# PixArt-style two-layer block on one core: first loads on two queues, and the second FFN's third and fourth elements prepared inside the last attention step

## The chip, the cores and the metric

The kernel runs on one core of one Trainium2 chip. The metric is the device time of one execution in microseconds (us). All data are float32; the matmuls run in float32 too.

## The reference

Sixteen batch elements of 256 tokens by 256 channels go through two layers. Each layer has self-attention, cross-attention and an FFN, each with a modulated layer norm ahead of it and a residual behind it. Cut to what matters:

```python
# layer 0 (16 heads of 64, rotary embedding on q and k; inner width 1024)
attn_in = adaln(x, cond, ...g1, b1)
x = attn(attn_in, attn_in, sa_wq, sa_wkv, sa_wo, sa_bo) + x
cross_in = adaln(x, cond, ...g1, b1)
x = attn(cross_in, ln(context), ca_wq, ca_wkv, ca_wo, ca_bo) + x
ffn_in = adaln(x, cond, ...g2, b2)
x = gelu(ffn_in @ ff_w1 + ff_b1) @ ff_w2 + ff_b2 + x
# layer 1 (16 heads of 16; six modulation vectors from silu(cond) @ Wmod + bmod)
x = x + attn_self(ln(x) * (1 + sc1) + sh1) @ Wos + bos
x = x + attn_cross(ln(x) * (1 + sc2) + sh2, context) @ Woc + boc
x = x + gelu((ln(x) * (1 + sc3) + sh3) @ W1 + b1) @ W2 + b2
```

Here `ln` is the layer norm over the last axis, `adaln(x, c) = ln(x) * (1 + c @ gw + gb) + (c @ bw + bb)`, and `attn` ends with the output product.

## The kernel before

Six phases run one after the other: layer 0's self-attention, cross-attention and FFN, then layer 1's. In each phase a loop runs over the 16 elements (`b`, a "job" each, whose key is phase_element); an attention job has two steps (`s` = 0, 1), an FFN job four. All of x stays in SBUF, one tile per element (`x0` to `x15`), and so do the weights of the running phase.

The order of work on every engine is the order in which the program issues it (`manual_schedule` for TensorE, VectorE, ScalarE, GpSimd and SyncE): each engine executes its own list in order, and waits in it for semaphores of the others. The short names of the profile are PE (TensorE's matmuls), PEld (its weight loads), DVE (VectorE), ACT (ScalarE), POOL (GpSimd), SP (SyncE, which issues the DMAs; ScalarE issues some too). DMAs share eight semaphores in turn, so that a DMA also waits for the landing of the one issued eight before it.

PSUM is one tile of eight banks, addressed by number. Attention steps of layer 1 use four banks from `at = 4 * s`: the next element's or the FFN's first products at `at`, the output product of the element before at `at + 1`, the two attention products (`layer1_sums`, e = 0, 1) at `at + 2` and `at + 3`. The FFN takes banks in turn by `next_bank()`; the first FFN product of phase 5 is put at bank 4 within the last attention step (`ffn_products`), and the ones after it take bank 7, 0, 1, 2 and so on.

How an element enters a phase, in four moves, each some steps ahead of its use:

- `prepare_moments`: mean and variance (VectorE: two L350, two L352, L354), and rstd by a power on GpSimd (L356).
- `prepare_norm`: `normalized` (VectorE, two L364 into the one buffer `xh`), then `turn` (two 32x32 stream transposes, L374, into `blocks`, and four DMAs, L379, that write `turned` to DRAM), then `add_bias` (GpSimd, two L452: the output bias is added to x).
- `prepare_fetch`: four DMAs (L389) that read `turned` back as `fetched`, transposed.
- `prepare_input`: `affine`, which applies the modulation to `fetched` and makes `hT` (chunk 0 on ScalarE, L422; chunk 1 on GpSimd, L426, or ScalarE, L424).

The layer-1 attention's softmax sums are inverted by `invert` (a VectorE reciprocal, L773), spread and multiplied in by `normalize` (VectorE L781, GpSimd L782); `finish` is the output product (TensorE, 16 products of four matmuls of 32 columns) and its addition to x (VectorE, L1044).

The FFN's elements 0 and 1 are computed plainly (`ffn_hidden`: 4 quarters of 16 products each). From element 2 on, pairs of elements (2 and 3, 4 and 5, ...) share a Strassen-like scheme of seven products: `fold_input` makes the four sums `inner` from both elements' hT (L839 to L842, for the first pair on VectorE), `block_products` uses them, and the output side uses sums of the weights, `output_w` (`fold_output_weights`, VectorE, L913 to L916, at element 1, step 2). All four sums need the hT of both elements.

The start: x0, the packed vectors `rows`, weights and tables are loaded by SP in one sequence; ScalarE's queue loads only the first modulation's weights. `condition` computes the sigmoid, transposes cond and `rows` on TensorE, with `idle_products` (matmuls of the identity that are not used) between them; then come the first modulation (L186 to L194), the first element's norm (`xh_first`), its four transposes, hT, and the first products of phase 0 (L82). Each of the two wk and wq loads of the `"first"` and `"last"` part covers half the heads; `load_first` is called between them and puts rope, the value weights, x1, x2, fold and mask after the first half.

## Time and profile before

| what | value |
|---|---|
| time, median of 3 runs | 2160.07 us (2159.74 to 2161.54) |
| profiled execution, its own time | 2160.07 us |
| its span, first to last instruction | 2158.3 us |
| PE busy | 2143.1 us (99%) |
| DVE, POOL, ACT busy | 1645.4, 1319.5, 877.6 us |
| mean granted TensorE clock | 0.999 |

The span is the stretch from the first to the last instruction; the time of an execution has 1.8 us more around it. A row of the order of time gives the start in us from the span's begin, the duration, engine, line, operation, out<-in tiles, shapes and count; neighbours of one kind are merged. In brackets stands how long the engine was idle before it and what ended that. Matmuls are pipelined, so that the next group can start before the last one's end. A product of the kernel appears as two matmuls per 32-column strip.

### The profile page before, as it was taken

To read this page: it belongs to the slowest core of one execution; us is meant where nothing else is said; L and a number is where in the kernel's file an instruction comes from. 1 tells how busy PE (TensorE), PEld (TensorE's weight loads), DVE (VectorE), ACT (ScalarE), POOL (GpSimd) and SP (SyncE) were. 2 spreads that over 40 slices of the span, in tenths; PEclk is the share of its full clock that TensorE was granted. 3 is DMA by queue.
4 is the path that set the end of the run, shared out by engine and by line. 5 is a ranking of instruction groups with operands and counts; after the bars stand their busy time and mean duration, and the time that the engine had idled before them with its cause. 6 is when DMAs were issued, how large, how long until landed. Compare 5 with 4: busy or idle time off the path is not lost.

```text
span 2158.3 us, 109746 instructions
## 1 busy us (share of the span) xinstructions
PE 2143.1 (99%) x50000; PEld 1423.2 (66%) x50000; DVE 1645.4 (76%) x3008; ACT 877.6 (41%) x1377; POOL 1319.5 (61%) x1234
## 2 busy tenths in 40 slices
PE   9999999999999999999999999999999999999998
PEld 5666666666666666666666678886566655656787
DVE  5877777777787889888888777865777777777865
ACT  3333333333323332333323333433666666664342
POOL 5867767767768777686776766662322233235773
PEclk9999999999999999999999999999999999999999
DMA  6110110110133221212212033221212232223221
GB/s 195 30 38 23 27 39 22 27 39 23 30 93 84 75 60 35 59 43 45 58 35 62 24 77 91 54 51 22 64 39 43 55 93 62 62 48 76 73 66 39
DMA packets 307027, 117.65 MB, mean 55 GB/s; under 512 B 243364, under 2 KB 289784, under 8 KB 306424
## 3 DMA queue, kind: packets, MB, share of 16 engines
q1 hardware_dynamic: 306008, 110.02, 20.5%
q8 instruction: 393, 6.44, 1.3%
q14 instruction: 82, 0.67, 0.1%
q10 hardware_dynamic: 544, 0.52, 0.1%
HBM read 77.14 MB, written 33.29 MB: 51 GB/s over the span
## 4 chain that ended last, share of the span: by engine, by line
PE 94%; DVE 2%; POOL 2%; DMA 1%; issue 1%; SPq 0%; ACT 0%; DVEq 0%; POOLq 0%; ACTq 0%
PE banks L82 60%; PE banks L657 16%; PE banks L724 10%; PE banks L740 5%; PE banks L593 2%; PE banks L502 1%; POOL qk L622 1%; POOL raw L713 1%; POOL folded L1003 0%; DVE x L957 0%; DMA spread<-sums_seen 0%; DVE m L614 0%; DMA rows<-in_rows 0%; POOL folded L926 0%; DMA turned<-blocks 0%
## 5 line engine op out<-in xcount | busy, mean ns | idle before, releaser
L670 ACT ACTIVATE pr<-banks 128x1024 f32<-128x1024 f32 x576 | 487.4, 938 | 423.4 <-PE banks L657 219.4
L622 POOL TENSOR_TENSOR qk<-m,m 128x512 f32<-128x512 f32 x256 | 378.4, 1498 | 214.6 <-DVE m L614 203.9
L614 DVE TENSOR_TENSOR m<-banks,rope 128x512 f32<-128x512 f32 x512 | 319.7, 678 | 33.9 <-PE banks L82 22.4
L676 DVE TENSOR_TENSOR both<-pr 128x1024 f32<-128x1024 f32 x128 | 169.4, 1323 | 101.8 <-ACT pr L670 100.1
L657 PE MATMUL banks<-qk 32*64 32x256 f32 x8192 | 239.5, 378 | 0.8 <-POOL qk L622 0.5
L724 PE MATMUL banks<-pr,v 128*32 128x256 f32 x4096 | 236.2, 379 | 0.0
L731 ACT COPY raw<-banks 128x512 f32<-128x512 f32 x128 | 75.1, 587 | 391.6 <-PE banks L724 379.4
L657 PEld LDWEIGHTS banks<-qk 32*64 32x64 f32 x8192 | 184.6, 131 | 59.8 <-issue 29.1
L724 PEld LDWEIGHTS banks<-pr,v 128*32 128x32 f32 x4096 | 133.4, 110 | 100.3 <-issue 16.8
L452 POOL TENSOR_TENSOR x<-x,bo_b 128x256 f32<-128x256 f32 x96 | 73.0, 779 | 164.8 <-DVE xh L364 164.8
L782 POOL TENSOR_TENSOR oT<-oT,spread 128x256 f32<-128x256 f32 x64 | 45.7, 735 | 206.5 <-DVE spread L781 206.5
L713 POOL TENSOR_TENSOR raw<-raw,spread 128x512 f32<-128x512 f32 x128 | 162.4, 1302 | 13.1 <-DMA spread<-sums_seen 13.1
L682 DVE STREAM_TRANSPOSE squares<-both 128x1024 f32<-128x1024 f32 x128 | 158.7, 1240 | 2.2
L689 DVE TENSOR_REDUCE rows<-squares 128x32 f32<-128x1024 f32 x128 | 155.1, 1212 | 1.7
L1003 POOL TENSOR_TENSOR folded<-raw,raw 128x512 f32<-128x512 f32 x90 | 141.8, 1604 | 2.4
L82 PE MATMUL banks<-hT,wk_sa 128*32 128x256 f32 x2048 | 134.7, 381 | 0.2 <-ACT hT L422 0.2
L82 PE MATMUL banks<-hT,wq_ca 128*32 128x256 f32 x2048 | 134.4, 379 | 0.0
L740 PE MATMUL banks<-pr,wide_v 128*32 128x256 f32 x2048 | 134.4, 379 | 0.0
L82 PE MATMUL banks<-hT,wq_sa 128*32 128x256 f32 x2048 | 133.9, 379 | 0.0
L657 PE MATMUL banks<-q,k 32*64 32x256 f32 x4096 | 128.3, 382 | 0.2 <-issue 0.2
L957 DVE TENSOR_TENSOR x<-banks,x 128x256 f32<-128x256 f32 (+2 forms) x150 | 79.6, 531 | 56.2 <-PE banks L82 49.8
L657 PEld LDWEIGHTS banks<-q,k 32*64 32x64 f32 x4096 | 87.5, 131 | 38.2 <-issue 14.3
(248 smaller groups left out, 4033.0 us busy)
## 6 DMA issues: line engine op xcount, KB each, us to landing
turned<-blocks SPq DMA_DIRECT2D x380, 64.0 KB
fetched<-turned SPq DMA_DIRECT2D x380, 64.0 KB
spread<-sums_seen SPq DMA_DIRECT2D x128, 128.0 KB
x<-in_x SPq DMA_DIRECT2D x16, 256.0 KB
fetched_c<-turned_c SPq DMA_DIRECT2D x64, 64.0 KB
cT<-in_ctx_turned SPq DMA_DIRECT2D x16, 256.0 KB
out<-x SPq DMA_DIRECT2D x15, 256.0 KB
ctx<-in_ctx SPq DMA_DIRECT2D x16, 192.0 KB
```

The source lines that it names most:

```text
L82: nc.tensor.matmul(out[cut], lhsT[:, cut], rhs, start=start, stop=stop, **more)
L614: nc.vector.tensor_tensor(m, pq, rope[:, s : s + 1, :].to_broadcast([P, 2, N]), ALU.mult)
L622: nc.gpsimd.tensor_tensor(r, x, y, (ALU.subtract, ALU.add)[out])
L657: nc.tensor.matmul(banks[64 * g : 64 * g + 64, at + h, t * N : (t + 1) * N], lhs, rhs, start=(half == 0 and (t == 0 or job["layer"] == 1)) ...
L670: nc.scalar.activation(pr[:, one], sc[:, one], AF.Exp, scale=0.125 if job["layer"] == 0 else 0.25)
L676: nc.vector.tensor_tensor(both, pr[:, :, 0, :], pr[:, :, 1, :], ALU.add)
L682: nc.vector.transpose(job["squares"].rearrange("p b k -> p (b k)"), job.pop("both").rearrange("p h n -> p (h n)"))
L689: nc.vector.tensor_reduce(job["rows"][:, u, :], job.pop("squares"), AX.X, ALU.add)
L713: nc.gpsimd.tensor_tensor(part, part, spread[:, u : u + 1, :].to_broadcast([P, 2, N]), ALU.mult)
L724: nc.tensor.matmul(o[32 * h : 32 * h + 32, half, :], v[:, t, col : col + 32], pr[:, h, t, :], start=(t == 0), stop=(t == NT - 1),)
L740: nc.tensor.matmul(o[32 * h : 32 * h + 32], v[:, t, 4 * c + h, 32 * e : 32 * e + 32], pr[:, h, t, :], start=(t == 0), stop=(t == NT - 1),)
L1003: eng.tensor_tensor(folded[m], *sums[m])
```

## The change

It has two parts.

The first loads. SP now issues cond, rows, x0, fold and mask. wk and wq of the first half and rope go to ScalarE's queue, issued by a call inside `condition`, behind the sigmoid and ahead of the exponential. The value weights, x1, x2, the second half of wk and wq, the output bias and weights and the other x tiles come on SP in this order, issued in the program after the first element's transposes. `xh_first` lies in the buffer of the value weights (`wpool`, tag `wv`) and not in `xh`; so the load of the value weights waits for the transposes that read it.

The border to the second FFN. In the last step of the last attention element (layer 1, s = 1, next is the FFN; `border`), `prepare_norm` of the FFN's element 2 and `prepare_moments` of its element 3 are issued after the first of the two attention products (e = 0) and not after both, or in the FFN's first step. In the FFN's element 0, step 0, element 3's norm, transposes and bias come first, and `invert` and `normalize` of the last attention element move to the end of step 1. The output product of that element (`finish(jobs[j - 2])`) moves from element 1's step 0 to its step 2, after that step's products.

On the engines' lists this means: PE has element 1's first 48 products in a row, then the 16 of the output product, then the last 16 of element 1. VectorE has element 2's norm and transposes and element 3's moments ahead of the last two reads of the second attention product (L754, L759, e = 1) and of the addition of element 14's output (L1044); the reciprocal comes after element 3's transposes, and the addition of element 15's output after element 4's norm and transposes. GpSimd has element 3's rstd ahead of element 1's hT, and element 3's bias ahead of `normalize`. SP writes element 3's `turned` before it fetches element 2's. The numbers of instructions on the engines stay the same, but for the three loads that move from SP to ScalarE.

```diff
-    def condition():
+    def condition(load):
         sig = work.tile([NB, D], F32, tag="inv", name="sig")
         nc.scalar.activation(sig, cond, AF.Sigmoid)
+        load()
...
-    def load_layer0_attention(kind, part, between=None):
+    def load_layer0_attention(kind, part, eng=nc.sync):
...
-            nc.sync.dma_start(out=wk, in_=wkv_src[:, :, halves[i]])
-            nc.sync.dma_start(out=wq, in_=chunked(a[f"{kind}_wq"])[:, :, halves[i]])
+            eng.dma_start(out=wk, in_=wkv_src[:, :, halves[i]])
+            eng.dma_start(out=wq, in_=chunked(a[f"{kind}_wq"])[:, :, halves[i]])
             w[f"wk{i}"], w[f"wq{i}"] = wk, wq
-            if between is not None and i == 0:
-                between()
...
-    def load_first():
-
-        nc.sync.dma_start(out=rope, in_=a["rope"])
-        load_phase(0, "values")
-        for b in range(1, 3):
-            load_x(b)
-        for dst, name in ((fold, "fold"), (mask, "mask")):
-            nc.sync.dma_start(out=dst, in_=a[name])
...
+    nc.sync.dma_start(out=rows, in_=a["rows"])
     load_x(0)
-    nc.sync.dma_start(out=rows, in_=a["rows"])
-    for part in ("first", "last", "early", "output"):
-        load_phase(0, part)
-    for b in range(3, NB):
-        load_x(b)
-    silu = condition()
+    for dst, name in ((fold, "fold"), (mask, "mask")):
+        nc.sync.dma_start(out=dst, in_=a[name])
+
+    def load_first():
+
+        load_phase(0, "first")
+        nc.scalar.dma_start(out=rope, in_=a["rope"])
+
+    silu = condition(load_first)
     jobs[0]["hraw"] = banks[:, 6:8, 0:N]
     found = moments(xs[0], "first")
-    xh = normalized(xs[0], found, D, "first")
+    xh = normalized(xs[0], found, D, "first", wpool, "wv")
...
+    load_phase(0, "values")
+    for b in range(1, 3):
+        load_x(b)
+    for part in ("last", "early", "output"):
+        load_phase(0, part)
+    for b in range(3, NB):
+        load_x(b)
     idle_products(2)
...
-            if b == 0 and s == (1 if layer0 else 0):
+            if b == 0 and s == 1 and layer0:
                 prepare_moments(third)
...
                 elif b == 0:
+                    prepare_norm(third)
                     prepare_fetch(after)
-                    invert(prev)
-                    third["turned"] = turn(
-                        normalized(xs[third["b"]], third.pop("moments"), D, third["key"]), 4, third["key"]
-                    )
-                    normalize(prev)
-                    add_bias(third)
-                if b == 1 and not layer0:
-                    finish(jobs[j - 2], next_bank())
...
+            if s == 1 and b == 0 and not layer0:
+                invert(prev)
+                normalize(prev)
             if s == 2:
+                if b == 1 and not layer0:
+                    finish(jobs[j - 2], next_bank())
...
+            border = nxt["kind"] == "ffn" and s == 1
             for e in range(2):
                 layer1_sums(job, s, e, at + 2 + e)
+                if border and e == 0:
+                    prepare_norm(third)
+                    prepare_moments(jobs[j + 4])
                 if s == 1:
                     finish(prev, at + 1, (e,))
...
             else:
-                prepare_norm(third)
+                if not border:
+                    prepare_norm(third)
                 prepare_input(after)
```

More of the change, by code (lines that the diff above doesn't have):

```diff
@@ L357, in moments, with normalized @@
         return mv, rstd
-    def normalized(src, found, width, name):
+    def normalized(src, found, width, name, pool=work, tag="xh"):
         mv, rstd = found
-        xh = work.tile([P, NT, width], F32, tag="xh", name=f"xh_{name}", bufs=1)
+        xh = pool.tile([P, NT, width], F32, tag=tag, name=f"xh_{name}", bufs=1)
         for t in range(NT):
@@ L1073, in fast @@
     phases = [
-        {"layer": 0, "kind": "attn", "cross": False, "load": lambda part: load_layer0_attention("sa", part, load_first),
+        {"layer": 0, "kind": "attn", "cross": False, "load": lambda part: load_layer0_attention("sa", part, nc.scalar if part == "first" else nc.sync),
          "mod_load": lambda: layer0_modulation(1)},
```

## The prediction

> **What bounds the kernel now.** I read the page first, then TensorE's waits, then the order of time on TensorE and VectorE around the two longest waits.

> ```profile
> PE 2143.1 (99%) x50000; PEld 1423.2 (66%) x50000; DVE 1645.4 (76%) x3008; ACT 877.6 (41%) x1377; POOL 1319.5 (61%) x1234
> ```

> TensorE (PE) is busy for 2143.1 of 2158.3 us. Both parts of the change add and remove no matmul, so they can give back only idle time, 15.2 us in all. Where it lies, the waits of PE tell (microseconds in total, times, longest):

> ```profile
> PE banks L82 <- DVE inner L840: 4.2, 1, 4.2
> PE banks L154 <- DMA rows<-in_rows: 1.3, 1, 1.3
> PE banks L138 <- POOL neg_half L93: 1.3, 1, 1.3
> ```

> The first lies at the start of the second FFN, the second and third in the first 6 us. The change touches the first and the second. PE's order of time at the start (start, duration, line, form, count, idle before):

> ```profile
> 3.02 1.22 PE L138 MATMUL banks<-ident 128*128 128x256 f32 x2
> 5.58 0.37 PE L154 MATMUL banks<-ident,rows 68*128 68x68 f32 x1 [1.34 <-DMA rows<-in_rows]
> 7.69 1.08 PE L186 MATMUL banks<-mod_a,condT 128*32 128x128 f32 x16
> 10.29 1.04 PE L138 MATMUL banks<-ident 128*128 128x256 f32 x4
> 11.48 0.85 PE L82 MATMUL banks<-hT,wk_sa 128*32 128x256 f32 x12 [0.15 <-ACT hT L422]
> ```

> PE is free at 4.24 and waits for rows until 5.58. All up to the first real product at 11.48 follows from there: modulation, its copy and transpose, five small VectorE steps, the affine hT.

> PE and its weight loads at the second FFN's start:

> ```profile
> 1948.44 1.05 PE L82 MATMUL banks<-wo_b,oT 128*32 128x256 f32 x16
> 1949.63 7.12 PE L82 MATMUL banks<-hT,w_b 128*32 128x256 f32 x128
> 1956.86 2.19 PE L82 MATMUL banks<-wo_b,oT 128*32 128x256 f32 x32
> 1958.87 6.23 PE L82 MATMUL banks<-hT,w_b 128*32 128x256 f32 x112
> ```
> ```profile
> 1949.63 3.40 PEld L82 LDWEIGHTS banks<-hT,w_b 128*32 128x32 f32 x68 [0.62 <-DVE sums L759]
> ```

> The reader is to see two things. PE stops when the line at 1958.87 ends, 1965.09, until the folded inputs are there at 1969.28. And at 1949.63 it already waits for VectorE's L759: the FFN's second quarter for element 0 is written to bank 7, where the last attention product (layer1_sums, e=1, bank at+3 with at=4) lies until L759 has read it. VectorE (DVE) at that place:

> ```profile
> 1949.10 0.47 DVE L759 SCALAR_TENSOR_TENSOR sums<-banks,mask,sums 128x256 f32<-128x256 f32 x1
> ...
> 1950.17 0.72 DVE L364 TENSOR_SCALAR xh<-x,mv,rstd 128x256 f32<-128x256 f32 x2
> ...
> 1952.46 0.28 DVE L354 TENSOR_SCALAR ve<-mv 128x2 f32<-128x2 f32 x1
> 1952.65 1.74 DVE L773 RECIPROCAL sums<-sums 128x256 f32<-128x256 f32 x1
> ...
> 1959.12 0.69 DVE L1044 TENSOR_TENSOR x<-banks,x 128x512 f32<-128x512 f32 x1 [1.60 <-PE banks L82]
> ...
> 1961.06 1.23 DVE L913 TENSOR_TENSOR output_w_L_xcond_b<-w_b 128x512 f32<-128x512 f32 x1
> ...
> 1968.80 0.43 DVE L840 TENSOR_TENSOR inner<-hT,inner 128x256 f32<-128x256 f32 x1
> ```

> **Part 1, the first loads.** rows goes ahead of x0 on SP's queue, issued at 1.18 instead of 1.64. By the landings in the trace cond (issued 0.72, same queue) took 1.9 us, x0 3.4 us (to 4.63), rows 3.9 us (to 5.54, behind x0's 256 KB). With 34 KB and only cond ahead, rows needs between 1.9 and 3.0 us and is there by 3.1 to 4.2. PE reaches L154 at 4.24, so the whole 1.34 us goes. The value is 1.34; bounds 0.9 (rows still dragged) and 1.34 for this step.

> What is late next: x0, now issued at 1.64. If it keeps its 3.45 us it lands at 5.1. The moments and the norm take from 6.14 to 8.94 today, 2.80 us, so xh would be complete at 7.9. PE's transposes of it begin at 9.43 today, 8.09 after the change: covered by 0.2 us, and 0.3 us more lie between the transposes' end (10.47) and the last addend (10.77).

> The three loads put on ScalarE's queue (wk, wq, rope) are issued behind the sigmoid, from about 3.1 us, at 0.45 to 0.49 us each as its two loads today: done at 4.6, then the table load (1.28) and the exponential (0.20), 6.1; the modulation's copy needs ScalarE at 7.5 (8.84 less 1.34). No cost. wk and wq landed at 8.36 and 10.07; they are needed at 10.1 and 11.0. They start a microsecond later but have the same bytes ahead and no longer the values, rope and x1 interleaved. No cost, 0.5 us if wq slips to 11.5. SP's next load, the values, waits for the last transpose (xh lies in their buffer), about 9.1, and with it wait x1, x2 and all later loads. Values took 1.28 us per 512 KB (12.01 to 13.29); 2 us of latency and two such transfers give 13.7, x1 14.3. PE wants the values at 17.0 (18.42 today), VectorE wants x1 at 15.0 (16.42). Covered. SP's first turned block stands behind thirteen x loads that end at 23.9 to 24.5; element 1's hT came at 35.86 and PE wants it at 39.42, a cover of 3.6 us against at most 2.

> The clock: the same idle product took 0.5 us a piece from 5.75 and 0.26 from 10.29 (4 in 1.04), and the change falls near 10.07. With the gap gone PE is dense from 3.02 on, not 5.58. I add 0.1 us (0, if the fast clock comes when it did, to 0.4, if it comes before the modulation; then x0 ends the stage). [...]

> Part 1: 1.34 + 0.1, **1.4 us gained** (0.9 to 1.7).

> **Part 2, elements 2 and 3.** Element 2's norm and element 3's moments move ahead of the last half step's two reads of bank 7 (L754, L759). On VectorE that is 9 instructions: two L364, two L374, two L350, two L352, one L354. Today they run from 1950.17 to the reciprocal's start at 1952.65, 2.48 us. Their inputs are there after L759 of e=0, which ends at 1947.96: rstd of element 2 is ready at 1947.48. So they run 1947.88 to 1950.36, L754 and L759 follow (0.40 start to start, then 0.47) to 1951.23, and PE begins at 1951.29 instead of 1949.63. **The moved work sits in front of what frees bank 7: 1.66 us lost** (the 0.73 us that VectorE idles ahead of L754 today, for PE's e=1 product, is filled by it and taken off already).

> Then PE runs without a stop: element 0's 48 products, 48 of element 1, at 0.108 us (7.12 less 0.19 for the last one's tail, over 64) to 1961.66. The output product of the last attention element (16 products, 1.73) ends at 1963.39; with the tail 1963.58. Its operand, normalized by POOL behind the reciprocal, is ready near 1956.7: cover 5 us. Today that product waits for POOL; 0.3 us ahead of it and 0.28 inside vanish, which this count holds already. 24 products more, and PE stands at the folded inputs at 1965.98.

> What is late next is VectorE. It adds that output (L1044, 0.07 us after PE's tail: 1963.65), 0.60 to the next, then L913 to L916. L913 took 1.23 us beside POOL's adds of L452 and the like ones behind it 0.69; POOL has nothing left to do then, so I take 0.69: L913 1964.25 to 1964.94, L914 from 1964.97, L915 1965.58, L916 1966.18, the first inner sum 1966.79 to 1967.21, the second 1967.24 to 1967.66; PE at 1967.72. [...]

> The DMAs: SP issues element 2's four blocks at 1949.3 (2.63), element 3's at 1953.2 (2.6), element 2's fetch at 1955.9 (1.70), element 3's when its last block has landed. A block took 2.1 to 3.7 us: 1957.7 to 1959.0. Fetched (1.7, and 1.9 for the last): 1961 to 1962.2. ScalarE makes element 3's hT behind its GELUs and element 2's hT, by 1964.8; VectorE wants it at 1966.79. Two us of cover, so L379's earlier place gives nothing beyond this.

> Part 2: 1969.28 less 1967.72, **1.56 us gained** (0.9 to 2.0); without the wait on bank 7 it would be 3.2.

> **Sum.** Nothing behind either place has a fixed date: the rest of the chain is PE itself. The profiled execution took 2160.07 us (span 2158.3 and 1.8 around it) and is also the median of the three (2159.74 to 2161.54). 2160.07 - 1.4 - 1.56 = **2157.1 us**.

> **Rivals.** (a) VectorE gets to L759 at once, or the FFN's second quarter does not have to wait for it. Then part 2 gives 3.2 and part 1 1.4: 2155.5. For it: releasers are inferred, and a copy of ScalarE could be the true one; against: the weight load starts 0.06 us after L759 ends, and bank 7 is the one written next. 0.12. (b) The values come late. Their two loads need PE's transposes and stand alone on SP. They took 9.69 us from first issue (3.60) to landing (13.29); the same from 9.1 ends at 18.8, 1.8 late. They decide above 10.9 us, when the delay passes the 2.96 gained; at 12.5 us they land at 21.6, 4.6 late: 2161.7. For it: x1 and all else queue there too; against: today's 9.69 were spent behind wk, wq and rope. 0.05. (c) DMA stays last at the FFN: two landings of 3.7 us and late fetches, hT 2 us past 1964.8 and 1.6 more, part 2 gives nothing: 2158.7. 0.05. (d) rows still drags, part 1 gives half: 2157.8. 0.05. The forecast keeps 0.73.

> **How the numbers follow.** What can be told from no change here is 0.2%, 4.3 us: 2155.8 to 2164.4. The forecast, (c) and (d) lie inside. Faster by more needs (a), or both parts at their upper end with a quick run: 0.14. Slower by more needs (b) at twice its price: 0.03. The rest, 0.83, is the same. Range: low end both parts at their best with the runs' scatter below (2160.07 - 3.7 - 0.7 = 2155.6, next to (a)), high end both at their least with the scatter above (2160.07 - 1.8 + 0.7 = 2158.9, past (c)).

> **What would show it.** L154 right behind the idle product near 4.24 with no DMA wait; the first L82 near 10.1. At the FFN a PE wait of about 2 us on the sums near 1949.9 in the new time (the 1951.3 above less 1.4), and the wait on inner down from 4.2 to about 1.7, with ScalarE's hT done before VectorE gets to inner. Wrong if that first wait is missing (then (a)), if inner waits for hT again (c), or if PE waits between 10 and 46 us for values or qk (b).

## The result, and the profile after

| what | before | changed |
|---|---|---|
| median of 14 runs each, same chip | 2160.41 us (2158.57 to 2162.24) | 2156.15 us (2154.98 to 2159.69) |
| ratio of the changed kernel to the one before | | 0.9981, 95% interval 0.9973 to 0.9990 |
| profiled execution, its own time and span | 2160.07, 2158.3 us | 2156.18, 2154.4 us |

The change takes 4.3 us off (interval 2.2 to 5.8), 0.19%. The prediction said 3.0. The first line is the page's line of busy times, the second fence the waits of TensorE (PE), in us in total, times and longest.

```profile
PE 2140.8 (99%) x50000; PEld 1425.4 (66%) x50000; DVE 1644.1 (76%) x3008; ACT 878.0 (41%) x1377; POOL 1321.6 (61%) x1234
```
```profile
PE banks L82 <- DVE sums L758: 1.7, 1, 1.7
PE banks L82 <- DVE inner L839: 1.6, 1, 1.6
PE banks L138 <- POOL neg_half L93: 1.3, 1, 1.3
PE banks L82 <- ACT hT L421: 0.6, 1, 0.6
```

The 4.2 us on `inner` have become 1.6, and the 1.3 us on `rows` are gone. Two waits are new: 1.7 us on the sums (bank 7) and 0.6 us on an hT of ScalarE. PE is also busy 2.3 us less with the same 50000 matmuls; no wait explains that. PE's order of time, after:

```profile
4.04 0.32 PE L155 MATMUL banks<-ident,rows 68*128 68x68 f32 x1
...
9.89 1.07 PE L82 MATMUL banks<-hT,wk_sa 128*32 128x256 f32 x16
...
38.62 7.07 PE L82 MATMUL banks<-wv_sa,hT 128*32 128x512 f32 x64 [0.61 <-ACT hT L421]
...
1949.93 10.57 PE L82 MATMUL banks<-hT,w_b 128*32 128x256 f32 x192 [1.68 <-DVE sums L758]
1960.32 1.91 PE L82 MATMUL banks<-wo_b,oT 128*32 128x256 f32 x32
1962.05 2.77 PE L82 MATMUL banks<-hT,w_b 128*32 128x256 f32 x48
1966.43 1.93 PE L82 MATMUL banks<-inner,input_w_L_xcond_b 128*32 128x256 f32 x32 [1.62 <-DVE inner L839]
```

And VectorE's (DVE):

```profile
1949.41 0.47 DVE L758 SCALAR_TENSOR_TENSOR sums<-banks,mask,sums 128x256 f32<-128x256 f32 x1
...
1962.30 0.69 DVE L1043 TENSOR_TENSOR x<-banks,x 128x512 f32<-128x512 f32 x1 [4.61 <-PE banks L82]
1962.90 0.68 DVE L912 TENSOR_TENSOR output_w_L_xcond_b<-w_b 128x512 f32<-128x512 f32 x1
...
1965.95 0.43 DVE L839 TENSOR_TENSOR inner<-hT,inner 128x256 f32<-128x256 f32 x1
```

The border runs as forecast: L758 late, then no stop, then the addition, four folded weights and two sums on VectorE, and PE behind them. In the kernel before the same 32 matmuls on `inner` took 3.42 us, not 1.93 (order of time, before):

```profile
1969.28 3.42 PE L82 MATMUL banks<-inner,input_w_L_xcond_b 128*32 128x256 f32 x32 [4.19 <-DVE inner L840]
```

Why, the busy times by stretch tell. Columns: stretch, length, busy time and count of PE, PEld, DVE, ACT, POOL, the granted TensorE clock, the DMA share, GB/s. Before:

```profile
1966.15:1969.56 3.41, 0.28 (x8) 0.20 (x12) 1.19 (x4) 1.92 (x5) 0.00 (x0) 1.00 0.56 112
1969.56:1972.97 3.41, 3.41 (x40) 1.69 (x36) 3.19 (x11) 0.36 (x1) 1.32 (x2) 0.50 0.14 37
1972.97:1976.38 3.41, 3.41 (x100) 2.75 (x96) 1.69 (x3) 0.84 (x2) 3.33 (x4) 1.00 0.68 168
```

```profile
1962.96:1966.37 3.41, 1.86 (x36) 0.86 (x28) 3.27 (x8) 1.83 (x4) 0.00 (x0) 1.00 0.14 26
1966.37:1969.78 3.41, 3.35 (x64) 2.06 (x68) 3.10 (x12) 0.48 (x2) 0.97 (x2) 1.00 0.59 135
```

So the two profiled executions differ as follows, by how much earlier the same PE instruction starts after the change (the lead on the kernel before): 1.6 us at 11.5; 0.80 at 39.4, behind the wait on hT; 0.33 at 64.8, because the 80 matmuls on `qk` ahead of it took 2.94 us where the kernel before took 2.49; 1.24 at 1756, because the execution before stood still here and there for 0.3 to 0.5 us (other kernels' executions show this against it too, so it is not the change); -0.31 at 1949.6, behind the wait on the sums; 2.85 at the products on `inner`; 4.53 when the clock is equal again; 3.9 at the end. The border thus gives 2.85 - 1.24 = 1.6, the clock 4.53 - 2.85 = 1.7, the start 0.3.

What slowed the matmuls on `qk` near 60 us isn't shown. They took 2.94 us in one other kernel below too (loads, idle products too late), 2.50 in the one with late x and 2.51 in the one with the values free. The wait of 0.25 us on `qk` behind them stands in the kernel before too.

### The profile page after: what moved, and what is told of

It is laid out like the page before. It is cut to its first block, busy times and chain, and to the rows that moved or that the text cites. A ratio compares the mean times of both kernels' runs of the same rounds, so it can differ in the third digit from the quotient of the medians.

```text
span 2154.4 us, 109748 instructions
## 1 busy us (share of the span) xinstructions
PE 2140.8 (99%) x50000; PEld 1425.4 (66%) x50000; DVE 1644.1 (76%) x3008; ACT 878.0 (41%) x1377; POOL 1321.6 (61%) x1234
## 4 chain that ended last, share of the span: by engine, by line
PE 93%; DVE 2%; POOL 2%; DMA 1%; SPq 1%; issue 1%; ACT 0%; DVEq 0%; POOLq 0%; ACTq 0%
PE banks L82 59%; PE banks L656 16%; PE banks L723 9%; PE banks L739 5%; PE banks L592 2%; PE banks L501 1%; POOL qk L621 1%; POOL raw L712 1%; DMA x<-in_x 0%; DVE m L613 0%; SPq L120 0%; POOL folded L1002 0%; DVE x L956 0%; DMA spread<-sums_seen 0%; DMA turned<-blocks 0%
## 5 line engine op out<-in xcount | busy, mean ns | idle before, releaser
L451 POOL TENSOR_TENSOR x<-x,bo_b 128x256 f32<-128x256 f32 x96 | 73.3, 783 | 161.8 <-DVE xh L363 161.8
L82 PE MATMUL banks<-hT,wk_sa 128*32 128x256 f32 x2048 | 134.7, 381 | 0.1
L82 PE MATMUL banks<-hT,wq_ca 128*32 128x256 f32 x2048 | 133.9, 379 | 0.0
L82 PE MATMUL banks<-hT,wq_sa 128*32 128x256 f32 x2048 | 133.9, 379 | 0.0
```

What stands on the lines that cost most here:

```text
L82: nc.tensor.matmul(out[cut], lhsT[:, cut], rhs, start=start, stop=stop, **more)
```

## The experiments

Each kernel was timed beside the kernel before on one chip. A ratio below is the kernel to the kernel before, with its 95% interval.

| kernel | median us | before us | ratio |
|---|---|---|---|
| changed | 2156.15 | 2160.41 | 0.9981 [0.9973, 0.9990] |
| first loads only | 2162.07 | 2160.44 | 1.0006 [0.9997, 1.0016] |
| border only | 2156.21 | 2160.44 | 0.9981 [0.9971, 0.9990] |
| rows first | 2159.61 | 2160.44 | 0.9998 [0.9988, 1.0007] |
| 18 idle products | 2162.00 | 2160.44 | 1.0007 [0.9998, 1.0017] |
| 8 idle products | 2158.96 | 2159.43 | 1.0001 [0.9992, 1.0011] |
| loads, idle products too late | 2165.09 | 2160.68 | 1.0016 [1.0007, 1.0025] |
| loads, 8 idle products | 2160.97 | 2160.81 | 1.0002 [0.9993, 1.0011] |
| changed, reads first | 2154.43 | 2159.43 | 0.9979 [0.9969, 0.9989] |
| changed, reads and weights | 2154.68 | 2159.43 | 0.9977 [0.9968, 0.9987] |
| changed, late x | 2154.59 | 2159.43 | 0.9978 [0.9968, 0.9987] |
| changed, values free | 2157.22 | 2160.68 | 0.9984 [0.9975, 0.9993] |
| changed, all three | 2154.02 | 2160.68 | 0.9969 [0.9957, 0.9981] |

### Each part by itself

The kernel before with the first loads alone:

```diff
+    nc.sync.dma_start(out=rows, in_=a["rows"])
     load_x(0)
-    nc.sync.dma_start(out=rows, in_=a["rows"])
...
+    silu = condition(load_first)
...
+    xh = normalized(xs[0], found, D, "first", wpool, "wv")
```

> The kernel before with the first part of the change alone (first loads, xh_first in the values' buffer). Theory: the first real product starts 1.6 us earlier (9.9 instead of 11.5), but the x loads end 3 us later on SP, element 1's first block goes out near 27.9 instead of 24.6, and TensorE waits 0.6 us for ScalarE's hT at 38.6 and some 0.4 us more for qk before 65: of 1.6 us only 0.3 to 0.5 are left, the span is 0.3 to 0.8 us under that of before. Rival: the shifts after 39 us in the changed kernel's trace are jitter of one execution, and all 1.6 us stay: no wait for hT at 38.6, span 1.6 us shorter.

Its first product on real data starts at 9.92 (11.48 before), with a wait of 0.5 us on hT at 38.5. Then the gap at the border. PE's order of time and the stretches of this kernel:

```profile
1968.56 3.64 PE L82 MATMUL banks<-inner,input_w_L_xcond_b 128*32 128x256 f32 x32 [3.70 <-DVE inner L839]
1971.97 1.90 PE L82 MATMUL banks<-hT,w_b 128*32 128x256 f32 x16
```
```profile
1963.48:1966.89 3.41, 1.38 (x28) 0.53 (x20) 0.50 (x1) 0.67 (x2) 0.00 (x0) 1.00 0.37 96
1966.89:1970.30 3.41, 1.74 (x20) 0.82 (x24) 2.57 (x9) 2.29 (x5) 0.00 (x0) 0.50 0.35 63
1970.30:1973.71 3.41, 3.41 (x40) 1.57 (x36) 2.01 (x5) 0.00 (x0) 2.69 (x4) 0.50 0.56 115
```

The wait is shorter than before's, 3.70 for 4.19, yet the half clock lasts 6.8 us. PE's lead on the kernel before falls from 0.72 us at `inner` to -0.12 five us later. That is not all of it: the span, 2160.4, is 2.1 us longer than before's. Another 0.55 us are lost at 1979, where PE stands still and no engine explains it, and 1.4 us in the last 10 us of the execution, of which 1.2 lie behind PE's last matmul. The runs scatter over 6 us.

The kernel before with the border part alone:

```diff
+                if border and e == 0:
+                    prepare_norm(third)
+                    prepare_moments(jobs[j + 4])
...
             if s == 2:
+                if b == 1 and not layer0:
+                    finish(jobs[j - 2], next_bank())
```

> The kernel before with the second part of the change alone (the border to the second FFN). Theory: a wait of 1.7 us on VectorE's sums at 1951 and one of 1.6 us on inner near 1967.7 take the place of the one of 4.2 us, which makes 1.6 us; and since no wait is longer than 1.7 us the granted clock does not fall to half after it, which makes 1.3 us more: 2.9 us in all, first inner product 1.6 us earlier, 32 matmuls from there in 1.9 us and not 3.4. Rival: the 1 us that the changed kernel gained behind the border is jitter, and the part gives 1.6 us.

Its PE order of time:

```profile
1950.38 10.57 PE L82 MATMUL banks<-hT,w_b 128*32 128x256 f32 x192 [1.68 <-DVE sums L759]
...
1966.88 1.93 PE L82 MATMUL banks<-inner,input_w_L_xcond_b 128*32 128x256 f32 x32 [1.61 <-DVE inner L840]
```

Same two waits, a granted clock of 1.00 from 1963 to 1973, and the whole measured gain of the change: 4.2 us, with the wait on `rows` (1.5 us) still there. From 1756 to `inner` the lead on the kernel before grows by 1.61 us and in the five us behind it by 1.69, the half clock that is missing. The first loads add next to nothing to this (2156.15 for both parts).

### The clock behind the gap

If the idle time brings the half clock, idle work in the gap must keep the clock up. Products of the identity, whose result is not used, were put in the kernel before ahead of the products on `inner` (18, then 8):

```diff
             block_products(job, x, 1, True)
+            if job["last"] and job["b"] == 2:
+                for _ in range(8):
+                    nc.tensor.matmul(
+                        bank(3, 2, P), ident, ident.unsqueeze(1).to_broadcast([P, 2, P]), start=True, stop=True
+                    )
```

> The kernel before with 18 idle products of the identity (about 0.22 us each) put where TensorE waits 4.2 us for the folded inputs, ahead of the first inner product; they write a bank that is free and nobody reads them. Theory: the first inner product starts when it did, near 1969.3, but the granted clock stays at 1.0 there, the 32 matmuls from there take 1.9 us instead of 3.4, and the span is 1.3 us shorter although work was added. Rival: the clock plays no part, and the span is the same or up to 0.3 us longer.

An idle product appears in the trace as two matmuls, 0.43 us in all; the 18 were therefore twice as long as reckoned, 8.0 us, and ran past the gap. PE, with 18:

```profile
1964.47 8.04 PE L871 MATMUL banks<-ident 128*128 128x256 f32 x36
1972.43 1.93 PE L82 MATMUL banks<-inner,input_w_L_xcond_b 128*32 128x256 f32 x32
```

The products on `inner` come 3.15 us later than before and take 1.93 us, where they took 3.42 before; the mean granted clock of this execution is 1.000. Of the 3.15 us, 1.47 are left behind them, and the median is 1.6 above before: the half clock was worth 1.7 us.

> The kernel before with 8 idle products (16 matmuls of 0.216 us, 3.5 us) in the wait of 4.2 us, in place of the 18 of the run before, whose 36 matmuls took 7.9 us and filled more than the wait. Theory: the first inner product starts as in the kernel before, 0.7 us behind the idle ones, the granted clock stays at 1.0 and the 32 matmuls from there take 1.9 us; the span is 1.4 to 2.6 us shorter than with the clock at half, and the runs scatter less than those of before. Rival: the clock plays no part, the span is as before.

PE, with 8:

```profile
1963.51 3.72 PE L871 MATMUL banks<-ident 128*128 128x256 f32 x16
1967.40 1.93 PE L82 MATMUL banks<-inner,input_w_L_xcond_b 128*32 128x256 f32 x32 [0.17 <-DVE inner L840]
```

The profiled execution shows the theory: the 32 products in 1.93 us instead of 3.42, `inner` not delayed, 1.69 us more lead behind it, span 2156.6. The medians do not confirm it: 0.5 us under before, with an interval from -1.7 to +2.4 us. One standstill of 1.5 us in the same trace, at 1980, which no engine explains, is as large as the effect.

The same with the first loads in, to spare the longer stretch. In the first attempt the idle products stood one line lower, behind `block_products(job, y, 6, True)`, and so behind the wait.

> The kernel before with part 1 (first loads) and eight idle products in the gap ahead of the folded inputs, which fill about 3.7 us of it. Theory (the loads alone were not faster because TensorE's 3.7 us wait there was followed by 6.8 us at half clock, which cost about 2.6 us): the records show full clock from 1960 to 1980, the 32 products on inner take 1.93 us instead of 3.42, the span is 2156.3 to 2157.5 and the median 2158 to 2159, 2 us or more under the 2162.1 of the loads alone. Rival (the half clock is a mark in the records and not the reason, the loads lose their time elsewhere): median 2161 or more.

PE in that kernel:

```profile
1969.00 1.93 PE L82 MATMUL banks<-inner,input_w_L_xcond_b 128*32 128x256 f32 x16 [3.87 <-DVE inner L839]
1970.86 5.61 PE L871 MATMUL banks<-ident 128*128 128x256 f32 x16
```

It says nothing of the question. It does show the price of the half clock once more: 16 matmuls on `inner` take as long as 32 do elsewhere, 16 idle ones 5.61 us instead of 3.72, with the half clock on for 6.8 us. The second attempt:

> The kernel before with part 1 (first loads) and eight idle products ahead of the first 32 products on inner, one product call earlier than in the run before this, where they stood behind the first 16 and so behind the wait. They fill 3.7 us of the gap. Theory (what the loads gain at the start is spent again by the half clock that follows TensorE's 3.7 us wait): the 32 products take 1.93 us instead of 3.4, the records show no half clock between 1960 and 1980, the span is 2155.5 to 2158 where the loads alone had 2160.4, and the median is 2157 to 2159.5, at least 2 us under the loads alone (2162.1). Rival (the half clock is a mark in the records and not what costs, or the loads lose their time at other places): the median stays at 2161 or more.

```profile
1962.91 3.72 PE L870 MATMUL banks<-ident 128*128 128x256 f32 x16
1967.17 1.93 PE L82 MATMUL banks<-inner,input_w_L_xcond_b 128*32 128x256 f32 x32 [0.53 <-DVE inner L839]
```

In PE's order of time all is as the theory has it, the granted clock is 1.00 from 1964.6 to 1971.4, and the span, 2156.4, lies where it put it. But this execution (2158.22) is the fastest of eleven; the median, 2160.97, is 1.1 us under the loads alone (1.5 with each set against its own runs of before), under the 2 us that the theory asked and not clearly apart from zero. Neither side won.

The executions that were not profiled have their mean granted clock on record, to three digits. One stretch of 3.41 us at half clock takes 0.0008 off that mean (1.7 of 2158.3 us), so that an execution at 1.000 has no room for one. (A lower mean says less, since half clock behind PE's last matmul counts in it too: before, that matmul ends at 2152.8, and the clock is 0.50 from 2157.3 to the end of the span.) Of the 99 executions of the kernel before that were timed beside these kernels none reached 1.000, and none of the 31 of the three others that keep the long wait (first loads only, rows first, idle products too late). Of the border alone 7 of 10 did, of the changed kernel 5 of 14, with 18 idle products 5 of 10, with 8 of them 2 of 10, with the loads and 8 of them 3 of 11. So it is not peculiar to the profiled executions that the half clock is gone where the wait is short or filled. With the loads alone, the seven executions at 0.998 or 0.997 took 2161.3 us or more, the three at 0.999 at most 2160.3.

The three at 1.000 of the last kernel took 2158.49, 2161.20 and 2162.31 us: what the longer two lost was not lost at half clock. Its profile shows one other place. PE's lead is 3.8 us at 2146, but the span is only 1.8 us shorter than before's: it ends 7.45 us behind PE's last matmul. That stretch is 6.66 us with the first loads only, 7.06 with the idle products too late, and 5.3 to 6.0 in the eleven other profiled executions. The three long ones are the three kernels that have the first loads and not the border; why their ends take longer is not known.

### The start

The kernel before with `rows` ahead of x0 on SP's queue, and nothing else:

```diff
+    nc.sync.dma_start(out=rows, in_=a["rows"])
     load_x(0)
-    nc.sync.dma_start(out=rows, in_=a["rows"])
```

> The kernel before with rows ahead of x0 on SP and nothing else moved. Theory: the wait of 1.34 us on rows is gone, the first real product starts between 9.9 and 10.3; the x loads keep their places, element 1's first block goes out near 24.6, and no wait for hT follows at 38: 1.3 to 1.6 us stay. Rival: without the move of wk and wq to ScalarE's queue x0 shares its time with them and lands after 5.5, so that the first product starts after 10.5 and less than 1 us is gained.

The first product starts at 10.09, and 1.06 us of lead are there at 64 us, without a wait on hT at 38. The gap at the border is there as before (4.52 us), and the 32 products behind it take 3.27 us (3.42 before); 0.8 us in the median can't be told from no change.

Next, why the changed kernel waits for hT at 38.6. Its DMA issues on SP:

```profile
13.86 13.68 SPq L120 DMA_DIRECT2D x<-in_x  x13
27.89 3.76 SPq L378 DMA_DIRECT2D turned<-blocks  x4
```

before the change:

```profile
13.99 10.27 SPq L120 DMA_DIRECT2D x<-in_x  x13
24.63 3.49 SPq L379 DMA_DIRECT2D turned<-blocks  x4
```

Element 1's turned block goes out 3.26 us later, since the thirteen loads of x3 to x15 stand ahead of it on SP, and their issue ends at 27.5 and not at 24.3. And these do so because the values, with all behind them, wait for PE's transposes until 8.9, with little left to move meanwhile. The stretch from 8 to 10 us, after and then before (DMA share and GB/s at the end):

```profile
8.00:10.00 2.00, 1.63 (x12) 1.18 (x16) 1.58 (x8) 0.56 (x1) 0.00 (x0) 1.00 0.47 167
```
```profile
8.00:10.00 2.00, 1.94 (x22) 1.39 (x15) 1.22 (x5) 0.27 (x1) 0.17 (x1) 1.00 0.99 369
```

The changed kernel with the loads of x3 to x15 issued behind element 1's turned block and its fetch:

```diff
     for part in ("last", "early", "output"):
         load_phase(0, part)
-    for b in range(3, NB):
-        load_x(b)
...
     prepare_fetch(jobs[1])
+    for b in range(3, NB):
+        load_x(b)
```

> The changed kernel with the loads of x3 to x15 behind element 1's turned blocks and fetch on SP, and nothing else moved. Theory: element 1's blocks go out as soon as SP has issued the output weights and VectorE is done with them, near 21 to 22 us and not at 27.9, TensorE does not wait for hT at 38, and of the 1.6 us of the start 1.2 more are kept than in the changed kernel. Rival: the x loads then keep element 2's blocks or the x tiles from coming in time, and the wait appears further on; no change of the span by 0.5 us.

SP and PE there:

```profile
22.60 2.69 SPq L378 DMA_DIRECT2D turned<-blocks  x4
26.96 2.68 SPq L388 DMA_DIRECT2D fetched<-turned  x4
29.68 7.58 SPq L120 DMA_DIRECT2D x<-in_x  x13
```
```profile
37.89 7.05 PE L82 MATMUL banks<-wv_sa,hT 128*32 128x512 f32 x64
```

No wait on hT; PE is 0.73 us ahead of the changed kernel at 38 and 1.18 us at 64. The median is 4.8 us under before, where the changed kernel had 4.3: in the right direction, not told apart.

The other way to fill the queues: the first norm in its own buffer again, so that the values wait for nothing.

```diff
-    xh = normalized(xs[0], found, D, "first", wpool, "wv")
+    xh = normalized(xs[0], found, D, "first")
```

> The changed kernel, but the first norm keeps its own buffer, so that the values' loads do not wait for TensorE's transposes of it. Theory (the DMA queues stood half idle from 6 to 14 us because everything on SP's queue stood behind the values, x loads ended 3 us later, element 1's turned block and hT with them): the windows at 8 to 14 us show over 350 GB/s again, element 1's turned block is issued near 24.6 instead of 27.9, TensorE has no wait on hT near 38, and about 1 us of the start is kept that the changed kernel gives back: 2155 to 2155.5 median. Rival (the values then share the queues with wk, wq and rope): wk or wq is there later than 9.4 us, the first real product starts past 10.5 instead of 9.89, and the median is 2156.2 or more.

PE, and the stretches:

```profile
10.91 1.07 PE L82 MATMUL banks<-hT,wk_sa 128*32 128x256 f32 x16 [1.18 <-DMA wk_sa<-in_sa_wkv]
12.74 1.57 PE L82 MATMUL banks<-hT,wq_sa 128*32 128x256 f32 x16 [0.76 <-DMA wq_sa<-in_sa_wq]
```
```profile
8.00:10.00 2.00, 1.52 (x8) 1.07 (x8) 1.56 (x8) 0.56 (x1) 0.00 (x0) 1.00 1.04 400
...
9.76:13.18 3.42, 1.51 (x24) 0.78 (x28) 0.04 (x1) 0.05 (x1) 0.00 (x0) 1.00 1.06 398
13.18:16.59 3.41, 3.41 (x36) 1.74 (x32) 1.29 (x2) 0.00 (x0) 0.00 (x0) 0.50 1.06 399
```

Both were right, and the rival decides. The queues are full (398 to 400 GB/s), the turned block goes out at 24.82, and nothing waits at 38. But wk and wq now share the transfers with the values and come 1.18 and 0.76 us late, and the granted clock is 0.50 for 3.41 us behind these two waits. PE is 2.08 us behind the kernel before at 15 us. The wait of the values for the transposes, which costs at 38 us, is also what brings wk and wq in time.

### The border

The changed kernel with element 2's norm and element 3's moments behind both reads of bank 7:

```diff
-                if border and e == 0:
+                if border and e == 1:
```

> The changed kernel, but with element 2's norm and element 3's moments behind the two reads of the second attention product (e = 1) in the last step, and ahead of the addition of element 14's output. Theory: the wait of 1.7 us on VectorE's sums is gone (0.1 to 0.3 us left); all behind it on TensorE moves up, the output product and its addition too, and the wait on inner stays at 1.6 us; span 1.4 to 1.7 us under that of the changed kernel. Rival: element 3's DMAs, now about 0.8 us later, end last, the wait on inner grows by what the other one lost, and nothing is gained.

```profile
1948.24 10.57 PE L82 MATMUL banks<-hT,w_b 128*32 128x256 f32 x192
...
1964.74 1.94 PE L82 MATMUL banks<-inner,input_w_L_xcond_b 128*32 128x256 f32 x32 [1.62 <-DVE inner L839]
```

The wait on the sums is gone, and `inner` comes 1.69 us earlier than in the changed kernel, behind an unchanged wait of 1.62. It is therefore the moved work in front of L758 that costs 1.7 us at bank 7. The medians, 5.0 us under before here and 4.3 for the changed kernel, do not tell the two apart.

To this, the output weights folded a step earlier (element 1, step 1):

```diff
+            if s == 1 and b == 1 and not layer0:
+                fold_output_weights(job["phase"], nc.vector)
...
-                    fold_output_weights(job["phase"], nc.vector)
-                    if not layer0:
+                    if layer0:
+                        fold_output_weights(job["phase"], nc.vector)
+                    else:
```

> As the run with the reads first, and the four sums of output weights on VectorE (L912 to L915) issued in element 1's step 1, behind element 4's norm, where VectorE is idle for 4.6 us in the changed kernel. Theory: the wait on inner, which VectorE's four sums end, goes from 1.6 us to 0 to 0.5, when hT of element 3 (ScalarE, behind the fetch) ends it; span 2.9 to 3.3 us under that of the changed kernel. Rival: ScalarE's hT was as late as the sums of weights, and the wait on inner stays above 1 us with hT as what ended VectorE's wait.

```profile
1963.17 1.93 PE L82 MATMUL banks<-inner,input_w_L_xcond_b 128*32 128x256 f32 x32 [0.74 <-DVE inner L839]
```

The wait halves, so VectorE's chain did set it; what ends VectorE's wait is now ScalarE's hT. In the median nothing more is seen than with the reads alone.

All three edits in the changed kernel (reads first, weights earlier, late x):

> The changed kernel with three edits together: the moved norm and moments behind both reads of bank 7 (e == 1), the output weights folded a step earlier, and x3 to x15 loaded behind element 1's turned block and fetch. Theory (the three costs stand at separate places and add): TensorE has no wait on the sums near 1949, at most 0.8 us on inner, none on ScalarE's hT near 38; from the profiles alone 0.7 us for the loads, 1.7 for the reads and 0.9 for the weights, 3.3 us under the changed kernel's 2156.2, so 2152 to 2153.5 median, and no stretch at half clock. Rival (one start earlier than another collides with the next bound, the fetch of elements 2 and 3 or the folded weights on VectorE): the inner wait is over 1.5 us again, ended by hT, and the median is 2154 or more, no better than the single edits.

PE, then ScalarE (ACT):

```profile
1963.17 1.93 PE L82 MATMUL banks<-inner,input_w_L_xcond_b 128*32 128x256 f32 x32 [1.60 <-DVE inner L839]
```
```profile
1961.53 0.60 ACT L421 ACTIVATE hT<-fetched,add_b,fac_b 128x256 f32<-128x256 f32 x1 [2.23 <-DMA fetched<-turned]
```

The rival holds: PE arrives earlier, but element 3's fetch does not, and hT, which waits for it 2.23 us, ends the wait on `inner` again. The median is 6.7 us under before and the lowest of all kernels tried; against the changed kernel the intervals of the two ratios still touch (0.9957 to 0.9981 and 0.9973 to 0.9990).

## Why the prediction was right, and where it was not

The time (2157.1 forecast, 2156.15 measured) lay in the range, and the gain of 0.19% just inside the 0.2% that was called no change, with an interval that reaches past it. By its steps:

- **The wait on `rows`, 1.34 gone and 0.1 for the clock: right.** L155 at 4.04 (forecast near 4.24), the first real product at 9.89 (10.1), 1.59 us earlier. Of these 1.55 are there at L155 already; the trace's record of the granted clock begins at 7.12, before at 10.31 (10.07 in the prediction's reading of the matmuls), and the four transposes of the first norm took 0.66 us instead of 1.04; that gave 0.04, not 0.1.
- **What the start keeps: wrong.** The step that failed is the cover "of 3.6 us against at most 2" for element 1's hT. It took SP's thirteen x loads to end about when they did; they ended 3.26 us later, as the queues moved 167 GB/s instead of 369 while the values waited, and PE stood 0.61 us on hT. Of 1.4 us forecast, 0.8 were left behind that wait and, after the slower matmuls on `qk`, 0.3 at 64.8 us in the profile. In the medians they gain nothing in any of the three pairs of kernels with and without them, each set against its own runs of before: added to the border part they change nothing (0.03 us), to the kernel before they cost 1.6 us, to the one with 8 idle products 0.6. No one of these can be told from none. In the profiles part of the last two lies at the end of the execution (1.2 and 1.8 us more behind PE's last matmul).
- **Bank 7, 1.66 lost: right.** PE waits 1.68 us there, and its lead falls by 1.55; that the moved work is the cause, the kernel with the reads first shows. Rival (a), that VectorE gets to L759 at once, fell.
- **The wait on `inner`, 1.56 gained, ended by VectorE: right.** 1.6; the wait that is left was forecast at 1.74 and is 1.62. L912 took 0.68 us with GpSimd idle (0.69 forecast); in the kernel with the weights folded earlier it fell beside GpSimd's addition of L451 and took 1.22, the two prices that were weighed. ScalarE had element 3's hT at 1963.37, 2.1 us before VectorE wanted it, the cover that was named; the kernel with all three edits shows what comes when that cover is used up, which is rival (c).
- **The sum: one term was missing.** "Nothing behind either place has a fixed date: the rest of the chain is PE itself" took PE's speed behind the gap as given, and so did "they can give back only idle time, 15.2 us in all": PE's busy time fell by 2.3 us with the same matmuls. In the kernel before PE ran at half clock for 3.41 us behind the 4.19 us wait; behind the 1.62 us wait of the changed kernel the clock is 1.00, and 1.7 us more are gained in the profiled executions. The rows were there to see: 3.42 us for 32 matmuls that take 1.9 elsewhere.
- **Rivals (b) and (d)** fell: the values landed at 14.90, and nothing waited for them; `rows` was there when PE was.

So 2.96 forecast was made of 1.4 at the start and 1.56 at the border; the 3.9 of the profiled executions are 0.3 at the start, 1.6 at the border, 1.7 by the clock, 0.9 of standstills that the profiled execution before happened to have, less 0.6 lost behind 1973. The missing term (1.7 more) and the lost start (1.1 less) nearly cancel: that the time came out so close is luck.

What stays open: that the half clock costs 1.7 us is shown in the profiled executions and by the 18 idle products, and the mean clocks of the other executions fit it, while the 8 idle products, which should have gained as much, gained 0.5 (interval 1.7 gained to 2.4 lost) without the first loads and 1.5 with them. Nor is it known why the ends of the three kernels with the loads and without the border take longer.

## What to carry to other kernels

A wait of TensorE can be worth more than its length: behind those of 3.70 to 4.52 us on `inner` 32 products took 3.27 to 3.64 us, behind those of 1.60 to 1.62 us 1.93 or 1.94. So look at the granted clock in the stretch behind a wait, and compare a group's duration there with the same group elsewhere. When a load is moved or gated, ask what the DMA queues do meanwhile and which transfer, far behind it on the same queue, comes later; and before work is moved ahead of a read, ask which bank that read frees. Once the first bound at a place is gone, edits there do not add: the next one (here a fetch) was 2 us away.

## What the runs showed of the hardware

Around PE's waits the profiled executions show this of the granted clock. The idle time is PE's, in the stretch named; the stretches are 3.41 us long (3.42 with the values free), and the clock in them is 1.00.

| kernel | stretch, us | idle in it, us | granted clock behind it |
|---|---|---|---|
| before | 1966.15 to 1969.56 | 3.13 | 0.50 for 3.41 us, then 1.00 |
| first loads only | 1963.48 to 1966.89 | 2.03 | 0.50 for 6.82 us, then 1.00 |
| loads, idle products too late | 1964.47 to 1967.88 | 2.75 | 0.50 for 6.83 us, then 1.00 |
| changed, values free | 9.76 to 13.18 | 1.91 | 0.50 for 3.41 us, then 1.00 |
| changed | 1962.96 to 1966.37 | 1.55 | 1.00 |
| changed, late x | 1944.58 to 1947.99 | 1.67 | 1.00 |

In the two kernels with 6.8 us at half clock PE was idle for another 1.67 and 1.12 us at the start of it; in the two with 3.41 us it was busy throughout. These are single stretches: what sets the clock, and why it stayed at half for 3.41 us here and for 6.8 there, they do not show. An estimate of the loss is half of PE's busy time at half clock: 1.7 us for the 3.41 of the kernel before, 2.6 us for the 1.74 + 3.41 with the first loads only. The mean clocks of the executions with the first loads only lie between 0.997 and 0.999.

The start varied too. The kernel with the idle products too late has the same first loads as the one with the first loads only, yet its four idle products ahead of the first product on real data took 1.91 us instead of 1.03, the first 16 of those products 1.57 instead of 1.07, and they started at 10.97 instead of 9.92. Its next two groups begin at 12.37 and 13.23, where the kernel before has them at 12.37 and 13.24: all that the first loads bring was gone. Why is not known.
